# Two seams between three stages: a lasting staging buffer, an earlier load, batch norm in two steps, and a last group copied on chip

## The chip, the cores and the metric

The kernel runs on one core of a Trainium2 chip. A core has five engines with instruction streams of their own: PE (TensorE, matmuls; PEld is its weight load), DVE (VectorE), ACT (ScalarE), POOL (GpSimd) and SP (SyncE, which here only issues DMAs). Sixteen DMA engines move data between DRAM and SBUF. Matmul results go to PSUM. The metric is the device time of one execution in microseconds; the median of several runs is compared.

## The reference, cut to what matters

The input x is 16 x 192 x 64 x 64 in float32. A first block and a second layer are computed; all is float32.

```
h = layer_norm(x over channels)
projected, gate = split(conv1x1(h))            # 192 -> 2 * 192
projected = depthwise3x3(projected, dw_k)
scanned = mix of four decaying scans of projected (left, right, down, up)
local = depthwise3x3(projected, le_k)
mixed = (scanned + local) * sigmoid(gate)
bn = batch_norm(mixed over all images and pixels, per channel)
x = x + conv1x1(gelu(bn))
x = x + fc2(gelu(fc1(layer_norm(x))))          # 192 -> 768 -> 192
wt = tap weights from relu(batch_norm(mean(x over pixels) @ w1)) @ w2
out = depthwise3x3(x, wt per image and channel; 4 taps) + bias
```

The batch norm needs sums over all 16 images, so nothing after it can start for a channel before the gate product of that channel is complete for the whole batch. That divides the kernel into stages.

## The kernel before, in words

**Three stages.** Stage A (`n` from 0 to 63, `project` on line 471) normalizes and projects. A chunk is 512 pixels of an image pair; four chunks are a block, of which there are 16. It writes projected values and gates of a block into a staging buffer, 48 KB per partition, of which there are two (`stg`, line 427) used in turn. The values are stored to DRAM (`pg_d`, line 81) sorted by channel group, 24 groups of 8 channels; the groups are divided into four tensors (`PARTS`, line 46). Group 0 is copied straight into an SBUF buffer that stays (`pg_even`, `store_first`, line 495). While block b is projected, one part of block b-1 is stored in each of its four chunks (lines 535 to 540); the last block is stored after the loop (lines 548 to 551).

Stage B (lines 554 to 740) works by group, four channel pairs to a group, 96 pairs `k` in all. `load_pg` (line 568) brings a group of 4 MB into one of three buffers: `pg_even` for groups 0, 3, 6, ..., `pg_o0` for 1, 4, ... and `pg_o1` for 2, 5, .... For each pair, `depthwise` (line 579, PE) multiplies by banded matrices `dm`, `tables` and `scans` (ACT, DVE) run the vertical scans, `local` and `vertical` (PE, through `lmul`, line 629, with matrices `lm`) do the rest, and `gate` (line 659, DVE) multiplies by the sigmoid, overwrites the group's buffer and collects statistics by `bn_stats`. After a group's last pair, POOL stores the group to DRAM (`mixed_d`, line 673).

`batch_norm` (line 677) turns the statistics into a scale and a bias, for channels 0 to 127 at `k` = 76 and for 128 to 191 at the end. It has two halves: PE sums the means over partitions (`pm`), DVE forms squared deviations (`dv`); then PE sums these (`pq`), and DVE and ACT form scale and bias.

Stage C (line 969 on) works by chunks `n` of 512 pixels of an image pair. `load_y` (line 198) reads the gated values back from `mixed_d`; three pieces `t` (channels 0 to 127 of either image, and 128 to 191 of both). `unmix` (line 794) transposes them on DVE into `mx`, two buffers used in turn, `bn_gelu` (ACT) applies scale, bias and gelu, `out_proj` (PE, then DVE on line 827) adds the projection to x in the image buffer `ximg`; `center`, `squares` and `normalize` do the second layer norm, `first` and `second` the two fully connected layers. The first step is `n` = -3: a chunk is unmixed three steps before its `first`.

**Order.** Inside each stage the order of the instructions on every engine, SP's and POOL's DMA issues among them, is the order of the program text (`manual_schedule`). An engine runs its instructions in that order, and one that waits holds those behind it. Waits come from the data: a load of `mixed_d` waits for the store, a write into a buffer waits for what still reads it.

**Memory.** Buffers of an ended stage give their place to later ones. `pg_o0` lies on stage A's weights and inputs, `pg_o1` on a staging buffer; `wf2` (fc2's weights, line 100) holds stage A's raw weights until then; `ximg` lies on buffers of stage B.

Of the kernel before, what the change touches and what calls it, by code (L numbers as in the profile page):

```python
# [27 lines left out]
C = 192  # L28
HW = 64
# [16 lines left out]
PARTS = ((1, 6), (6, 12), (12, 18), (18, NCG))  # L46
# [8 lines left out]
def conv_block_kernel(ctx: ExitStack, tc: tile.TileContext, x, prm, w_in, w_out, w_fc1, b_fc1, w_fc2, w1, bn1, w2, out):  # L55
# [44 lines left out]
    wf2 = k2.tile([128, NFC, C], F32, tag="wf2", name="wf2")  # L100
# [72 lines left out]
    mats[0]["lm"] = lm_even  # L173
    bn_sc = cp.tile([128, 2], F32, tag="bn_sc", name="bn_sc")
# [9 lines left out]
    def load_lm(g):  # L184
        n = GC // 2
        for i, q in enumerate(HALF):
            v = lv_d[g, i, :, 0:1, :]
            src = bass.AP(v.tensor, v.offset, [[n, HW], [128 * n, 5], [1, HW * n]])
            (nc.sync, nc.gpsimd)[i].dma_start(mats[g % 2]["lm"][q].rearrange("p k m c -> p k (m c)"), src)
# [8 lines left out]
    def load_y(n, y, queues, ts=(0, 1, 2)):  # L198

        p, c = divmod(n, NCH)
        for t, q, i, c0 in ((0, slice(0, 128), 0, 0), (1, slice(0, 128), 1, 0), (2, HALF[0], 0, 128), (2, HALF[1], 1, 128)):
            if t in ts:
                nq = (q.stop - q.start) // 32
                ih, i8 = divmod(2 * p + i, n_half)
                v = mixed_d[i8, c // 2, HALF[ih]].rearrange("w g e -> w (g e)")[:, c0 * BR:(c0 + 32 * nq) * BR]
                for wh in range(2):
                    vw = v[32 * wh:32 * wh + 32].rearrange("w (q e) -> q w e", q=nq)
                    qd, k = (q, wh) if t < 2 else (HALF[wh], i)  # L210
                    if len(queues) == 1:
                        queues[0].dma_start(y[qd, t, k], vw)
                    else:
                        for b in range(nq):
                            p0 = qd.start + 32 * b
                            queues[b % 2].dma_start(y[p0:p0 + 32, t, k], vw[b])


    with ExitStack() as stage:
# [5 lines left out]
        w0 = wf2.rearrange("p m c -> p (m c)").rearrange("p (t n) -> p t n", t=3)  # L225
# [190 lines left out]
        for k in range(5):  # L416
            beside(40 + k, load_weights, k)
        beside(46, load_dm, 0)
        beside(47, load_lm, 0)
        beside(48, load_dm, 1)  # L420
        beside(50, lambda: finish_weights(0, bank()))
# [5 lines left out]
        stg = [stage.enter_context(tc.tile_pool(name=f"stg{i}", bufs=1)) for i in range(2)]  # L427
# [43 lines left out]
        def project(n):  # L471
            blk, part = divmod(n, per)
            if part == 0:
                both_i = stg[blk % 2].tile([128, 2, 2 * C, BR], F32, tag="stg", name="stg")
                stag[blk] = [both_i[:, i] for i in range(2)]
            for g in range(AR):
                ps = [psa.tile([128, 2 * C], F32, tag=f"pj{i}", name=f"ps_pj{i}", bufs=2) for i in range(2)]
                for t in range(3):
                    for i, q in enumerate(HALF):
                        nc.tensor.matmul(ps[i], pixels(n, t, g)[q], wi[q, t].rearrange("p g k c -> p (g k c)"),  # L480
                                         start=(t == 0), stop=(t == 2))
                if n + 1 < n_ac:
                    variance(n + 1, g)
                j, rs = part * AR + g, ast[n]["rs"]
                nc.vector.tensor_scalar_mul(stag[blk][0][:, :, j], ps[0], rs[:, g, 0:1])  # L485
                nc.scalar.activation(stag[blk][1][:, :, j], ps[1], AF.Copy, scale=rs[:, g, 1:2])  # L486
# [8 lines left out]
        def store_first(blk):  # L495

            for i, par, q, i8, b, qh in each(blk):
                (nc.gpsimd, nc.sync)[par].dma_start(pg_even[qh, i8 * NB + b].rearrange("p k c j -> p (k c j)"),
                                                    stag[blk][i][q, 0:2 * GC].rearrange("p o j -> p (o j)"))
# [7 lines left out]
        with tc.manual_schedule(engines=ORDER):  # L507
# [23 lines left out]
            for n in range(n_ac):  # L531
                if n + 3 < n_ac:
                    load_a(n + 3)
                blk, part = divmod(n, per)
                if blk:
                    if part == 0:
                        store_first(blk - 1)
                    store(blk - 1, part, (nc.gpsimd, nc.sync))
                    if part == per - 1:
                        stag.pop(blk - 1)  # L540
                if n + 1 < n_ac:
                    turn(n + 1)
                project(n)
                if n + 1 < n_ac:
                    deviation(n + 1)
                for f, args in side.pop(n, ()):
                    f(*args)
            store_first(blk)
            store(blk, 0, (nc.gpsimd, nc.sync))
            for d in range(1, len(PARTS)):  # L550
                store(blk, d, (nc.gpsimd, nc.gpsimd))


    with ExitStack() as stage:
        pg_odd = []
        kb = stage.enter_context(tc.tile_pool(name="kb", bufs=1))
        pg_odd.append(kb.tile([128, n_blk, 2, GC, BR], F32, tag="pg_o0", name="pg_o0"))
        wb = stage.enter_context(tc.tile_pool(name="wb", bufs=2))
        kc = stage.enter_context(tc.tile_pool(name="kc", bufs=1))
        late = {}  # L560
# [7 lines left out]
        def load_pg(g):  # L568
            s = grp[g]
            if g == 2:  # L570
                pg_odd.append(kc.tile([128, n_blk, 2, GC, BR], F32, tag="pg_o1", name="pg_o1"))
            s["pg"] = pg_even if g % 3 == 0 else pg_odd[g % 3 - 1]
            if g:
                d = [lo_ <= g < hi_ for lo_, hi_ in PARTS].index(True)
                lo_ = (g - PARTS[d][0]) * GE
                nc.sync.dma_start(s["pg"].rearrange("p n k c j -> p n (k c j)"),
                                  pg_d[d][:, :, :, lo_:lo_ + GE].rearrange("i b p e -> p (i b) e"))
# [51 lines left out]
        def lmul(k, m, src, dst, start, stop):  # L629
            g, c = divmod(k, hp_)  # L630
            for i, q in enumerate(HALF):
                for ih, o in enumerate(HALF):
                    nc.tensor.matmul(dst(bst[k]["ps"][i][o]), mats[g % 2]["lm"][q, m, :, c], src(q, ih), start=start, stop=stop)  # L633
# [25 lines left out]
        def gate(k):  # L659
# [10 lines left out]
            if c == hp_ - 1:  # L670

                for i0, i1 in ((0, n_half),) if g < NCG - 1 else ((0, 2), (2, n_half)):
                    nc.gpsimd.dma_start(mixed_d[i0:i1, :, :, g].rearrange("i b p e -> p (i b) e"),
                                        s["pg"][:, i0 * NB:i1 * NB, 0].rearrange("p n c j -> p n (c j)"))
                s.clear()

        def batch_norm(cls):

            chs = (slice(0, 128), slice(128, C))[cls]
            n = chs.stop - chs.start  # L680

            means = stats.rearrange("p c (e k) -> p k e c", k=3)[:, 1, :, chs]
            sums2 = stats.rearrange("p c (e k) -> p k e c", k=3)[:, 2, :, chs]
            dv = late["dev"][:, :, chs]
# [6 lines left out]
            nc.vector.scalar_tensor_tensor(dv, sums2, 2.0 / (n_half * HW), dv, ALU.mult, ALU.add)  # L691
            pq = psb.tile([128, CH], F32, tag="l", name="pq", bufs=4)
# [12 lines left out]
        with tc.manual_schedule(engines=ORDER):  # L705
            load_pg(0)
            load_pg(1)
            load_pg(2)
            mats[1]["lm"] = kc.tile([128, 5, HW, hp_], F32, tag="lm1", name="lm1")
            load_lm(1)  # L710
            late["dev"] = kc.tile([128, 2, C], F32, tag="dev", name="dev")
            for k in range(-2, n_bp + 1):
                if 0 <= k + 1 < n_bp:
                    tables(k + 1)
                if k >= 1:
# [3 lines left out]
                    if c == 0 and 0 < g < NCG - 1:  # L719
                        load_lm(g + 1)  # L720
                    if c == 0 and g + 2 < NCG:
                        load_pg(g + 2)
# [9 lines left out]
                if k == n_bp - 5 * hp_:  # L732
                    batch_norm(0)
# [5 lines left out]
            load_y(0, y_low, (nc.sync, nc.gpsimd), (2,))  # L739
            batch_norm(1)  # L740

# [52 lines left out]
    def unmix(n):  # L794

        c, y = n % NCH, ys[n // 2]
        mx = mxs[n % 2]
        r0 = (c % 2) * CR
        for t in range(3):

            kinds = ("p k (c j) -> p j k c", "p (r k w) -> p r k w") if t < 2 else ("p k (c j) -> p k j c", "p (k r w) -> p k r w")
            blocks = y[:, t].rearrange(kinds[0], j=BR)
            blocks = blocks[:, r0:r0 + CR] if t < 2 else blocks[:, :, r0:r0 + CR]
            nc.vector.transpose(mx[:, t].rearrange(kinds[1], k=2, w=32), blocks)  # L804
        st[n].update(mx=mx)
# [153 lines left out]
    def at(f, n, *a):  # L959
        if 0 <= n < n_ch:  # L960
# [8 lines left out]
    with tc.manual_schedule(engines=ORDER):  # L969
        for n in range(-3, n_ch + 1):  # L970
# [3 lines left out]
            if n == -3:  # L974
                border(ximg[0])
                nc.vector.memset(pool2, 0.0)
            if n == NCH - 3:
                border(ximg[1])
            at(load, n + 3)
            at(unmix, n + 3)  # L980
            at(load_mixed, n + 4)
            at(first, n, 0)
            at(bn_gelu, n + 3)
# [21 lines left out]
            at(second, n, 1)  # L1005

# [51 lines left out]
```

## Time and profile before

| | |
|---|---|
| median of 4 runs | 3883.9 us (3878.66 to 3886.72) |
| profiled execution | 3884.27 us |
| its span, first to last instruction | 3882.5 us |
| PE busy | 3793.3 us (98%) |
| DVE busy | 2596.9 us (67%) |
| ACT busy | 1775.1 us (46%) |
| POOL busy | 412.8 us (11%) |
| mean granted PE clock | 0.989 |

The profile records one execution. Times below are microseconds from the start of its span. A line such as `L589` is line 589 of the kernel; `ps_d<-pg_o,dm` is what an instruction writes and reads. In lists of waits, the engine that waits and its line come first, then what it waited for: total time, how many times, the longest. In lists in order of time, the columns are start, duration, engine, line, operation, `x` and the number of instructions merged, and in brackets the idle time before them with what ended it.

### The profile page before, as it was taken

What the parts mean: (1) busy time and instruction counts of PE and PEld (TensorE: products, weight loads), DVE (VectorE), ACT (ScalarE), POOL (GpSimd) and SP (SyncE); (2) the same over time, 40 slices, a digit from 0 to 9 for tenths busy, and PEclk for the clock granted to TensorE, in tenths of its full rate; (3) what the DMA queues carried; (4) which work ended last, traced back from release to release, by engine and by line L of the source; (5) the groups of instructions that cost most, each with busy time, mean ns of one, the idle gap of its engine ahead of it and who ended that gap; (6) DMA issues with size and microseconds to landing.
All of it is one profiled execution on the core that took longest, in us unless ns stands there. A gap on an engine that the chain in (4) does not pass through costs nothing.

```text
span 3882.5 us, 59908 instructions
## 1 busy us (share of the span) xinstructions
PE 3793.3 (98%) x24972; PEld 1728.6 (45%) x24972; DVE 2596.9 (67%) x3820; ACT 1775.1 (46%) x1879; POOL 412.8 (11%) x667
## 2 busy tenths in 40 slices
PE   8999999999999989999999999999999999999998
PEld 5566665555555433333333333333333333333333
DVE  6777777899999954446656656655665665664654
ACT  3333334788887733334333433433433433343432
POOL 2333332001010020000000000000000000000000
PEclk9999999999999989999999999999999999999999
DMA  6789987999999841112212212222222221221212
GB/s 156 228 246 245 276 256 256 256 283 274 279 278 254 215 87 35 39 41 66 80 44 67 69 59 63 60 64 59 68 55 63 71 63 44 80 70 41 68 28 71
DMA packets 305535, 491.03 MB, mean 126 GB/s; under 512 B 45344, under 2 KB 200208, under 8 KB 305264
## 3 DMA queue, kind: packets, MB, share of 16 engines
q1 hardware_dynamic: 246640, 290.58, 27.9%
q0 software_dynamic: 58208, 196.28, 18.8%
q8 instruction: 197, 3.23, 0.4%
q14 instruction: 74, 0.61, 0.1%
q10 hardware_dynamic: 416, 0.33, 0.0%
HBM read 284.98 MB, written 197.92 MB: 124 GB/s over the span
## 4 chain that ended last, share of the span: by engine, by line
PE 92%; DMA 4%; DVE 2%; issue 1%; ACT 0%; SPq 0%; POOL 0%; DVEq 0%; POOLq 0%; ACTq 0%
PE ps_f L870 27%; PE ps_f L775 25%; PE ps_pj L480 11%; PE ps_l L633 10%; PE ps_d L589 6%; PE ps_o L824 5%; PE ps_o L820 3%; PE ps_xt L455 2%; PE ps_v L775 1%; PE ps_m L775 1%; DMA pg_d<-stg 1%; DMA pg_o<-pg_d 1%; DMA dm<-dv_d 1%; DMA xa<-in_x_dram 1%; DMA out_dram<-ol 0%
## 5 line engine op out<-in xcount | busy, mean ns | idle before, releaser
L870 PE MATMUL ps_f<-h,wf 64*128 64x512 f32 x4608 | 1042.5, 598 | 3.1 <-DVE h L860 3.1
L775 PE MATMUL ps_f<-gl,wf 128*64 128x512 f32 x4608 | 1021.5, 592 | 0.0
L873 ACT ACTIVATE gl<-ps_f,bf 128x1024 f32<-128x1024 f32 x384 | 428.2, 1115 | 1182.9 <-PE ps_f L870 1182.1
L870 PEld LDWEIGHTS ps_f<-h,wf 64*128 64x128 f32 x4608 | 430.6, 187 | 611.8 <-issue 611.0
L827 DVE SCALAR_TENSOR_TENSOR ximg<-ps_o,pt,low 128x256 f32<-128x256 f32 x384 | 168.3, 480 | 748.6 <-PE ps_o L824 748.6
L775 PEld LDWEIGHTS ps_f<-gl,wf 128*64 128x64 f32 x4608 | 330.5, 137 | 580.0 <-issue 537.9
L480 PE MATMUL ps_pj<-wi,xa 64*128 64x384 f32 x3072 | 516.9, 489 | 5.8 <-DVE stg L485 5.7
L486 ACT ACTIVATE stg<-ps_pj,rsa 128x384 f32<-128x384 f32 x256 | 239.0, 939 | 377.3 <-PE ps_pj L480 347.5
L480 PEld LDWEIGHTS ps_pj<-wi,xa 64*128 64x128 f32 x3072 | 292.3, 188 | 202.6 <-issue 12.3
L67 DVE SCALAR_TENSOR_TENSOR o<-ximg,taps,o 128x1024 f32<-128x1024 f32 x252 | 323.5, 1284 | 84.9 <-ACT o L930 78.8
L934 POOL DMA_DIRECT2D out_dram<-o x168 | 88.2, 530 | 2158.0 <-DVE o L67 2155.4
L485 DVE TENSOR_SCALAR stg<-ps_pj,rsa 128x384 f32<-128x384 f32 x256 | 228.3, 892 | 103.0 <-PE ps_pj L480 85.6
L859 DVE RECIPROCAL rs<-rs 128x512 f32<-128x512 f32 x64 | 214.6, 3353 | 82.6 <-ACT rs L858 82.6
L624 DVE TENSOR_TENSOR_SCAN v<-tab,q 128x1024 f32<-128x1024 f32 x96 | 218.3, 2274 | 10.8 <-ACT tab L612 10.8
L626 DVE TENSOR_TENSOR_SCAN v<-tab,q 128x1024 f32<-128x1024 f32 x96 | 217.5, 2265 | 0.0
L824 PE MATMUL ps_o<-low,wo 128*64 128x256 f32 x1536 | 210.2, 395 | 0.0
L612 ACT ACTIVATE tab<-mask,dec_b 128x1024 f32<-128x1024 f32 x192 | 209.3, 1141 | 0.0
L891 DVE SCALAR_TENSOR_TENSOR ximg<-ps_f,pt,ximg 128x512 f32<-128x512 f32 x192 | 137.4, 749 | 92.3 <-PE ps_f L775 88.0
L589 PE MATMUL ps_d<-pg_o,dm 64*64 64x384 f32 (+2 forms) x2560 | 181.2, 426 | 14.9 <-DMA pg_o<-pg_d 14.6
L462 DVE BATCH_NORM_STATS2 st<-ps_xt 128x6 f32<-128x192 f32 x512 | 174.1, 340 | 24.0 <-PE ps_xt L455 24.0
L589 PEld LDWEIGHTS ps_d<-pg_o,dm 64*64 64x64 f32 x2560 | 123.4, 198 | 103.4 <-issue 75.2
L804 DVE STREAM_TRANSPOSE low<-low 128x512 f32<-128x512 f32 x174 | 167.4, 1015 | 0.0
(181 smaller groups left out, 3710.1 us busy)
## 6 DMA issues: line engine op xcount, KB each, us to landing
pg_o<-pg_d SPq DMA_DIRECT2D x16, 4096.0 KB
low<-in_x_dram SPq DMA_DIRECT2D x128, 384.0 KB
out_dram<-o POOLq DMA_DIRECT2D x168, 256.0 KB, 3.7
pg_d<-stg POOLq DMA_DIRECT2D x102, 384.0 KB, 7.5
pg_d<-stg SPq DMA_DIRECT2D x90, 384.0 KB
mixed_d<-pg_o POOLq DMA_DIRECT2D x15, 2048.0 KB, 11.8
low<-mixed_d SPq DMA_DIRECT2D x116, 256.0 KB
low<-pg_d SPq DMA_DIRECT2D x7, 4096.0 KB
```

The lines of the kernel that those rows point to most:

```text
L67: nc.vector.scalar_tensor_tensor(o, in0, scalar, in1, ALU.mult, ALU.add, **kw)
L480: nc.tensor.matmul(ps[i], pixels(n, t, g)[q], wi[q, t].rearrange("p g k c -> p (g k c)"), start=(t == 0), stop=(t == 2))
L485: nc.vector.tensor_scalar_mul(stag[blk][0][:, :, j], ps[0], rs[:, g, 0:1])
L486: nc.scalar.activation(stag[blk][1][:, :, j], ps[1], AF.Copy, scale=rs[:, g, 1:2])
L589: nc.tensor.matmul(dst(ps[o, ih]), mats[g % 2]["dm"][q, di + 1, :, ch], src(s["pg"][q, :, 0, ch]), start=(di == 0), stop=stop)
L624: nc.vector.tensor_tensor_scan(vf, tab, q, 0.0, ALU.mult, ALU.add)
L626: nc.vector.tensor_tensor_scan(vf[:, ::-1], tab[:, ::-1], q[:, ::-1], 0.0, ALU.mult, ALU.add)
L633: nc.tensor.matmul(dst(bst[k]["ps"][i][o]), mats[g % 2]["lm"][q, m, :, c], src(q, ih), start=start, stop=stop)
L775: nc.tensor.matmul(ps[q], w(i), rhs(i), start=start, stop=stop)
L824: nc.tensor.matmul(ps[q, wh].rearrange("p (r w) -> p r w", w=32), wo[:, 64 * t:64 * t + 64], cols(rows(s["mx"][:, i]))[:, :, wh], start=Fa ...
L870: nc.tensor.matmul(pf[:, i], wf1[q, t, 128 * m:128 * m + 128], s["h"][q, t], start=(t == 0), stop=(t == 2))
L873: nc.scalar.activation(gl, pf, AF.Gelu, bias=bf1[:, m:m + 1])
```

## The change

1. **Staging.** A buffer `mid` (48 KB per partition) lasts through stages A and B. It takes the blocks with odd numbers; even ones keep a buffer of stage A. In stage B, `mid` holds the buffer of groups 2, 5, 8, ... (formerly `pg_o1`), the `lm` matrices of odd groups and `dev`, the batch norm's deviations. The last group, 23, therefore lies in `mid`, and `ximg[0]` of stage C lies over it.
2. **Parts.** Group 1 becomes a part of its own: `PARTS` has five tensors. While the next block is projected, group 1 is stored with the first rows, and one of the other four parts in each chunk.
3. **Second group's load.** Of the last block only the first rows and group 1 are stored inside stage A, by POOL and ACT. Stage B then begins with `load_pg(1)`, images 0 to 5 of either half on SP and the rest on POOL; the other 16 stores of the last block follow on SP, then `load_pg(2)`.
4. **lm of group 1.** It is loaded during stage A into `place`, the memory that holds stage A's raw weights before and fc2's weights later; these are loaded at group 3.
5. **Batch norm.** `batch_norm` is split into `spread` (pm and dv) and the rest, which follows one pair later for the first 128 channels.
6. **End of stage B.** The transposes of chunk 0 move from stage C to the end of stage B, around `spread(1)` and `batch_norm(1)`. Chunk 0's third piece is read from DRAM without the last group, two pairs before the end; the last group's rows are copied from its SBUF buffer into `y_low` by four DMAs. The last group is stored with one DMA instead of two.
7. **Start of stage C.** The memset of `pool2` moves from `n` = -3 to `n` = 0. The transposes and the gelu of chunk 2 move from the start of step `n` = -1 to its end.

```diff
-PARTS = ((1, 6), (6, 12), (12, 18), (18, NCG))
+PARTS = ((1, 2), (2, 7), (7, 13), (13, 18), (18, NCG))
...
+    place = k2.tile([128, 5 * HW * (GC // 2)], F32, tag="place", name="place")
+    wf2 = place[:, 0:NFC * C].rearrange("p (m c) -> p m c", m=NFC)
...
+    SB_ = 2 * 2 * C * BR
+    mid = ce.tile([128, SB_], F32, tag="mid", name="mid")
+    mats[1]["lm"] = mid[:, NPG:NPG + 5 * HW * (GC // 2)].rearrange("p (k m c) -> p k m c", k=5, m=HW)
...
+    lm_first = place.rearrange("p (k m c) -> p k m c", k=5, m=HW)
+    lm_of = lambda g: lm_first if g == 1 else mats[g % 2]["lm"]
...
+                    if last < 32:
+                        for b, ncb in ((0, 32), (1, last)):
+                            p0 = qd.start + 32 * b
+                            queues[0].dma_start(y[p0:p0 + 32, t, k, 0:ncb * BR], vw[b, :, 0:ncb * BR])
...
+    def turn_back(y, mx, half, t):
+        kinds = ("p k (c j) -> p j k c", "p (r k w) -> p r k w") if t < 2 else ("p k (c j) -> p k j c", "p (k r w) -> p k r w")
+        blocks = y[:, t].rearrange(kinds[0], j=BR)
+        r = slice(half * CR, (half + 1) * CR)
+        nc.vector.transpose(mx[:, t].rearrange(kinds[1], k=2, w=32), blocks[:, r] if t < 2 else blocks[:, :, r])
...
-        for k in range(5):
+        for k in (0, 1, 3, 4):
             beside(40 + k, load_weights, k)
...
+        beside(49, load_lm, 1)
...
-                both_i = stg[blk % 2].tile([128, 2, 2 * C, BR], F32, tag="stg", name="stg")
+                if blk % 2:
+                    both_i = mid.rearrange("p (i o j) -> p i o j", i=2, j=BR)
+                else:
+                    both_i = stg.tile([128, 2, 2 * C, BR], F32, tag="stg", name="stg")
...
                     if part == 0:
                         store_first(blk - 1)
-                    store(blk - 1, part, (nc.gpsimd, nc.sync))
+                        store(blk - 1, 0, (nc.gpsimd, nc.sync))
+                    store(blk - 1, part + 1, (nc.gpsimd, nc.sync))
...
-            store_first(blk)
-            store(blk, 0, (nc.gpsimd, nc.sync))
-            for d in range(1, len(PARTS)):
-                store(blk, d, (nc.gpsimd, nc.gpsimd))
+            store_first(blk, (nc.gpsimd, nc.scalar))
+            store(blk, 0, (nc.gpsimd, nc.gpsimd))
...
-                for i0, i1 in ((0, n_half),) if g < NCG - 1 else ((0, 2), (2, n_half)):
-                    nc.gpsimd.dma_start(mixed_d[i0:i1, :, :, g].rearrange("i b p e -> p (i b) e"),
-                                        s["pg"][:, i0 * NB:i1 * NB, 0].rearrange("p n c j -> p n (c j)"))
+                if g == NCG - 1:
+                    for i in range(2):
+                        for wh in range(2):
+                            w0_ = 32 * wh
+                            (nc.sync, nc.gpsimd)[wh].dma_start(y_low[2 * w0_ + 32:2 * w0_ + 64, 2, i, LASTC * BR:],
+                                                              s["pg"][w0_:w0_ + 32, i * NB, 0].rearrange("p c j -> p (c j)"))
+                nc.gpsimd.dma_start(mixed_d[:, :, :, g].rearrange("i b p e -> p (i b) e"),
+                                    s["pg"][:, :, 0].rearrange("p n c j -> p n (c j)"))
...
             load_pg(0)
-            load_pg(1)
+            load_pg(1, nc.sync, 0, n_half - 2)
+            load_pg(1, nc.gpsimd, n_half - 2, n_half)
+            for d in range(1, len(PARTS)):
+                store(blk, d, (nc.sync, nc.sync))
             load_pg(2)
...
+                    if c == 0 and g == 3:
+                        load_weights(2)
...
                 if k == n_bp - 5 * hp_:
+                    spread(0)
+                if k == n_bp - 5 * hp_ + 1:
                     batch_norm(0)
...
-            load_y(0, y_low, (nc.sync, nc.gpsimd), (2,))
+                if k == n_bp - hp_ // 2:
+                    load_y(0, y_low, (nc.sync,), (2,), LASTC)
+            turn_back(y_low, mxs[0], 0, 0)
+            spread(1)
+            turn_back(y_low, mxs[0], 0, 1)
             batch_norm(1)
+            turn_back(y_low, mxs[0], 0, 2)
...
+            if n == 0:
                 nc.vector.memset(pool2, 0.0)
...
+            early_, late_ = (n + 3, None) if n != -1 else (None, 2)
             at(load, n + 3)
-            at(unmix, n + 3)
+            at(unmix, early_)
...
-            at(bn_gelu, n + 3)
+            at(bn_gelu, early_)
...
             at(second, n, 1)
+            at(unmix, late_)
+            at(bn_gelu, late_)
```

## The prediction

> **What bounds the kernel now.** I began with busy time by stage, cutting the span at the two seams (columns: length, then busy time and instruction count of PE, PE's weight loads, DVE, ACT, POOL; granted PE clock, DMA share, GB/s).
>
> ```profile
> 0.00:648.80 648.80, 625.67 (x3966) 392.45 (x3966) 478.37 (x1491) 250.73 (x336) 218.48 (x367) 1.00 0.85 233
> 648.80:1353.70 704.90, 675.48 (x7692) 374.44 (x7692) 668.34 (x584) 572.09 (x677) 79.25 (x85) 0.98 0.99 266
> 1353.70:1392.90 39.20, 18.95 (x126) 8.24 (x126) 25.00 (x37) 12.15 (x12) 21.50 (x37) 0.67 0.86 186
> 1392.90:3882.50 2489.60, 2473.24 (x13192) 953.43 (x13192) 1425.19 (x1709) 940.12 (x854) 93.54 (x179) 1.00 0.22 58
> ```
>
> The first and last rows are PE without gaps (626 of 649, 2473 of 2490 us): nothing but PE work could change them. The middle stage has PE and DVE close together, and the 39 us before the last stage are less than half filled. So I asked PE's waits, longest first:
>
> ```profile
> PE ps_d L589 <- DMA pg_o<-pg_d: 14.6, 1, 14.6
> PE ps_o L820 <- ACT low L810: 10.6, 1, 10.6
> ...
> PE pq L696 <- DVE dev L691: 6.3, 2, 5.6
> PE ps_v L775 <- DVE sm_sq L850: 5.6, 1, 5.6
> ```
>
> Four holes, one or two each; all lie at seams or at the batch norm. For the middle stage I then read DVE in order of time, since there a hole counts only if DVE, too, stands still:
>
> ```profile
> 679.99 2.27 DVE L626 TENSOR_TENSOR_SCAN v<-tab,q 128x1024 f32<-128x1024 f32 x1
> 697.59 0.69 DVE L667 TENSOR_TENSOR low<-ps_l,sg 128x512 f32<-128x512 f32 x1 [15.34 <-PE ps_l L633]
> ...
> 1204.33 2.27 DVE L624 TENSOR_TENSOR_SCAN v<-tab,q 128x1024 f32<-128x1024 f32 x1
> ...
> 1211.33 2.27 DVE L624 TENSOR_TENSOR_SCAN v<-tab,q 128x1024 f32<-128x1024 f32 x1
> ...
> 1224.77 2.27 DVE L624 TENSOR_TENSOR_SCAN v<-tab,q 128x1024 f32<-128x1024 f32 x1
> ...
> 1363.70 0.06 DVE L976 MEMSET pool<- 128x6 f32 x1 [5.23 <-DMA low<-mixed_d]
> 1363.80 5.66 DVE L804 STREAM_TRANSPOSE low<-low 128x512 f32<-128x512 f32 x6
> ```
>
> The scans start every 7.00 us (1204.33, 1211.33): that is DVE's period for a pair, without a gap, against PE's 6.89. DVE sets this stage; 96 x 7.00 = 672 us, and it lasts from 659.4 to 1353.7. The excess is the 15.34 us hole and the 13.44 us pair of the first batch norm (6.44 too long), with little else. At the second seam the last gate product ends at 1352.94, and DVE starts the transposes only at 1363.80, behind a memset that was let go with the last group's store. The chain of what ended last says where that time goes:
>
> ```profile
> 1353.26 7.82 DMA mixed_d<-pg_o x2
> 1361.08 4.16 DMA low<-mixed_d
> 1365.27 0.48 DVE low L804
> ```
>
> A round trip through DRAM, 12 us. The first hole has its own line on SP, whose load of group 1 waited for the last stores of that group:
>
> ```profile
> 649.81 1.23 SPq L504 DMA_DIRECT2D pg_d<-stg  x2
> 656.35 22.82 SPq L576 DMA_DIRECT2D pg_o<-pg_d  x2
> ```
>
> Issued at 656.35, it landed at 687.6, among the last block's stores (6.3 MB) and group 2's load.
>
> **What the skill says.** (1) "DMA: Bandwidth & Descriptors", section on the anatomy of one DMA: a DMA costs about 2.0 us plus bytes at 436 GB/s, most of the fixed part being the receipt of the last write. Trace: the 64 KB first-rows copies at 649.43 took 2.39 us; agrees. (2) Same page, "Issuing engines are not separate DMA queues": SP, ACT and POOL share the 16 engines, so moving stores from POOL to SP buys no bandwidth and costs none. Trace: SP's load alone moves 348 GB/s (687 to 694 us), both queues' stores about 370 (615 to 632); roughly agrees. (3) "TensorE: Matmul & The Clock Gate", section on the HAM clock gate: idle PE falls to half clock and needs about 3.4 us of work to recover. Trace: after the first hole 40 L589 matmuls took 5.36 us, elsewhere 2.61; agrees. DVE's 15.34 us already contain this.
>
> **The change, part by part.**
>
> *Group 1 ahead of the last stores.* Three quarters of the load (images 0 to 5 of each half, 3 MB) need nothing of the last block and only the memory of stage A's inputs, free at 648.7. It can go at about 649.3. Its own last stores (256 KB, POOL) land near 655, then POOL loads the last 1 MB. With 4.5 MB at some 350 GB/s (the rate of the seam between 652 and 694 us) that is 13 us: landed near 664. PE asks at 673.1 (687.73 - 14.6), DVE stalls only if depthwise(4) starts after 675.3 (scan 3 ends at 682.2, less 6.9 us of PE work before the next gate). Margin 11 us: gain 15.3.
>
> What is late next: group 2. Behind group 1 on SP stand 16 stores (5.8 MB), then group 2's load, which overwrites `mid` and so waits for all of them. 649.3 + (3 + 1 + 0.5 + 5.8 MB)/356 GB/s = 678; 2 us receipt; 4 MB at 348 = 11.5, 2 more: 694, or 697 if dm's halves come between. dm for group 2 follows on SP at about 698. PE asks at 673.1 + 27.6 = 700.7, DVE suffers from 703.3. Cover 3 to 7 us; I take 0, bounds 0 and +10. Group 3 comes after the store of group 0 (693 + 13), landed by 720, needed at 731. Hidden.
>
> *Staging, five parts.* 16 blocks x 4 = 64 more stores, half of them per queue: 2 x 0.61 us on SP and 2 x 0.55 on POOL in the first chunk of a block. SP is busy 8.7 us there (299.48 to 308.2), so about 9.9 against a chunk of 9.4, but its x loads are three chunks ahead. Same bytes; the last part's size and issue time, on which the buffer's return depends, stay. The load of lm for group 1 moves into stage A (0.65 MB), fc2's weights (0.59 MB, 1.7 us of DMA) move to group 3, behind about 10 us of slack. The first rows go by POOL and ACT instead of POOL and SP: ACT is idle until 656.75. All 0; bounds -2 and +8.
>
> *First batch norm in two steps.* Now PE waits 5.6 us for dv, and starts cold: two vertical passes took 3.70 instead of 1.89 us. With the pq products one pair later, PE goes on with vertical(76) and depthwise. DVE keeps the three dv operations (0.57 + 0.43 + 0.61, with gaps 1.75) and the five small ones (mv to bias: 0.16 + 0.36 wait + 4 x 0.2 = 1.3). Sum 3.1, and 0.1 of queueing: 3.2 instead of 6.44. Gain 3.2, bounds 1.5 and 4.7 (6.44 - 1.75: only dv left).
>
> *Second seam.* Counted from the end of the gate: statistics end at 1353.67; transpose t0 to 1354.65 (0.94 each, 6 in 5.66) while PE makes pm (ends 1354.9); dv 1354.94 to 1356.06 as before; t1 to 1357.1 beside pq; mv 1357.2, square root on ACT, scale and bias ready at 1358.47; t2 1358.5 to 1359.5. The four copies of 16 KB on chip, on SP and POOL, start at 1353.3; by (1) 2.04 us, say landed by 1356.5: no wait, and 2 us of cover. Group 22's rows are loaded long before. ACT: gelu table loaded at 1359.0, 1.2 us for t0 and t1, 0.8 for t2: PE starts at 1361.0 instead of 1367.78. Gain 6.8. Chunk 2's three transposes (2.9 us) leave the stretch between chunk 0's sums and its centering; PE's own order gives back 0.6 of it: gain 2.3. Then they stand behind normalize, beside 7 us of first(0,0); ACT takes chunk 2's gelu first, which may hold out_proj(2) by 0.4. Against it: `mid` now holds the last group and ximg[0] lies on it. The first write of ximg[0] (L827) would be ready at 1364.1; the store, issued at 1354.4 after POOL's two copies, lands some 10 us later (2 MB in 10.3 us before): 1364.4. Loss 0.3, bounds 0 and 4. Sum 6.8 + 2.3 - 0.4 - 0.3 = 8.4.
>
> *Sum.* 15.3 + 3.2 + 8.4 = 26.9 off 3882.5 us of span: 3855.6. The profiled execution took 3884.27 (1.8 around the span), 0.4 above the median of 3883.9, so **3857** for the median. The last stage is PE without gaps and passes the gain on.
>
> **Rivals.** *Group 2 late.* For: 0.99 DMA share, everything behind 16 stores on one queue, cover of 3 to 7 us. Against: 350 GB/s on that queue. If it lands at 708 to 713, 5 to 10 us are lost: 3862 to 3867. *The last stage pinned by ximg[0].* For: the memset at 1363.70 shows that a new buffer over the last group's memory waits for its store, and such stores took up to 13.7 us under load. Then L827 starts at 1368: 3861. *The early load isn't early*: it still waits for the last stores, because something of theirs lies in its memory or the load isn't split from them. Only 11.6 remain: 3872. *Slower: stage A's block boundaries.* A new block may write its staging only when the stores of two blocks ago have landed; at 292.10 such a store took 11.9 us against a lead of 9.4, and PE lost 1.1 us. Four more stores in a block, queued on SP ahead of the x loads and of later stores, could stretch this. Over 15 boundaries it decides from 26.9/15 = 1.8 us more each; at 2.5 us each the time is 3857 + 37 = 3894. Against: the stores that decide go out three chunks after the added ones, and from 530 us on boundaries cost nothing (9.40 us for each chunk).
>
> **How the numbers follow.** Forecast 0.62; group 2 late 0.13; pinned start 0.10; load not early 0.05; stage A longer 0.10, of which 0.07 end slower and 0.03 level. Faster 0.90, same 0.03, slower 0.07; a change under 0.2% (8 us) is about what a measurement of this kernel can't tell from none. The range: down, 5 us beyond the forecast's gains (its bounds: 1.5 at the batch norm, 2 in stage A, the rest at the seams) and 2 for the spread of runs, 3850; up to 3868, which takes in the first two rivals. That holds about 0.82.
>
> **What would show it.** Right: no wait of L589 for pg_o near 675, scans every 7 us through groups 1 and 2; the batch-norm pair near 10.2 us; 8 us from the last gate product to out_proj, 31 to first(0,0). Wrong: L589 waiting at the start of group 2; L827 waiting for the store; stage A over 650 us; a load of group 1 that starts after 655.

## The result: three gains arrived, two new waits took them back

The kernel after takes 3886.43 us (median, 3880.29 to 3891.55) against 3884.02 us (3877.62 to 3892.33) for the kernel before in the same comparison: a ratio of 1.0005, 95% interval 1.000 to 1.001. Nothing was gained. The forecast was 3857.

The totals hide that much moved. Five marks that every trace here has cut the span: the last block of stage A (start of PE's first depthwise matmuls), the first scan on DVE, the moments' matmul `pm` that follows the last gate product, the first matmul of `first(0, 0)`, and the end.

| us | stage A | last block to first scan | stage B: first scan to `pm` | `pm` to `first(0,0)` | to the end | span |
|---|---|---|---|---|---|---|
| before | 648.76 | 10.65 | 694.41 | 39.04 | 2489.64 | 3882.5 |
| after | 648.83 | 17.33 | 693.79 | 31.48 | 2489.97 | 3881.4 |
| forecast | 648.8 | 10.65 | 675.9 | 30.6 | 2489.6 | 3855.6 |

The forecast's row is the row of before less 15.3 and 3.2 in stage B and 8.4 at the second seam. Stage A and stage C are as foreseen. The first seam is 6.7 us too long, stage B 17.9 and the second seam 0.9. The table also makes the experiments readable: the stretch called stage A differed between 644.7 and 655.1 us from one execution to the next, also in kernels whose stage A is the same, so effects of a few microseconds are read below from a stretch and not from the whole time.

**The hole before group 1 is gone.** DVE's scans in order of time in the kernel after (start, duration, engine, line), where before had its wait of 15.34 us at 682.2:

```profile
677.54 2.27 DVE L648 TENSOR_TENSOR_SCAN v<-tab,q 128x1024 f32<-128x1024 f32 x1
...
684.54 2.28 DVE L648 TENSOR_TENSOR_SCAN v<-tab,q 128x1024 f32<-128x1024 f32 x1
...
691.54 2.27 DVE L648 TENSOR_TENSOR_SCAN v<-tab,q 128x1024 f32<-128x1024 f32 x1
...
698.55 2.27 DVE L648 TENSOR_TENSOR_SCAN v<-tab,q 128x1024 f32<-128x1024 f32 x1
```

A pair every 7.00 us, also where group 1 begins (its first gate product is at 702.92) and, further on, group 2, which came in time. The first batch norm, same view, answers to before's 7.00, then 13.44:

```profile
1202.68 2.27 DVE L648 TENSOR_TENSOR_SCAN v<-tab,q 128x1024 f32<-128x1024 f32 x1
...
1211.35 2.27 DVE L648 TENSOR_TENSOR_SCAN v<-tab,q 128x1024 f32<-128x1024 f32 x1
...
1219.53 2.27 DVE L648 TENSOR_TENSOR_SCAN v<-tab,q 128x1024 f32<-128x1024 f32 x1
...
1226.53 2.27 DVE L648 TENSOR_TENSOR_SCAN v<-tab,q 128x1024 f32<-128x1024 f32 x1
```

Two pairs of 8.67 and 8.18 us: 2.85 us more than two plain pairs, where before had 6.44 and 0.14 more. A gain of 3.7.

**Two new waits.** The list of PE's waits after (what waits, for what: total, times, longest) has two that before had not:

```profile
PE ps_l L657 <- DVE pg_o L691: 12.8, 1, 12.8
PE ps_d L613 <- DMA pg_d<-mid: 8.4, 1, 8.4
...
PE ps_o L857 <- ACT low L847: 5.4, 1, 5.4
```

The first is in stage B, at the start of group 22, the last but one. DVE's instructions there, in order of time:

```profile
1289.55 2.27 DVE L648 TENSOR_TENSOR_SCAN v<-tab,q 128x1024 f32<-128x1024 f32 x1
1291.74 2.27 DVE L650 TENSOR_TENSOR_SCAN v<-tab,q 128x1024 f32<-128x1024 f32 x1
1310.56 1.03 DVE L240 STREAM_TRANSPOSE low<-low 128x512 f32<-128x512 f32 x1 [16.55 <-DMA low<-mixed_d]
1311.52 0.65 DVE L691 TENSOR_TENSOR pg_o<-ps_l,sg 128x512 f32<-128x512 f32 x1
...
1314.13 2.27 DVE L648 TENSOR_TENSOR_SCAN v<-tab,q 128x1024 f32<-128x1024 f32 x1
...
1332.50 1.04 DVE L240 STREAM_TRANSPOSE low<-low 128x512 f32<-128x512 f32 x1
```

L240 is `turn_back`, a transpose that brings gated values into stage C's layout. The kernel's text has chunk 0's three behind the last gate product, and that is where four more run, from 1359.72 on. So the two here are taken to be chunk 1's, which the kernel's text has in stage C (`unmix(1)`, step `n` = -2); e1 below bears this out. Here one stands between a pair's scans and its gate product, and waits 16.55 us for a load of gated values; the chain of what ended last gives that load, and the store that it waited for:

```profile
1289.38 11.76 DMA mixed_d<-low
1301.22 0.64 SPq L228
1301.92 8.51 DMA low<-mixed_d
```

From scan to scan 24.58 us went by (1289.55 to 1314.13) instead of 7.00: 17.6 lost. The second transpose costs its own 1.0.

The second wait is at the first seam. All engines and queues in order of time:

```profile
648.71 1.28 ACTq L526 DMA_DIRECT2D low<-mid  x2
648.79 0.40 SPq L600 DMA_DIRECT2D pg_o<-pg_d  x1
...
648.83 1.14 PE L613 MATMUL ps_d<-low,dm 64*64 64x512 f32 x4 [1.12 <-ACT mid L514]
648.97 1.06 POOL L526 DMA_DIRECT2D low<-mid  x2 [28.28 <-DVE mid L513]
649.24 19.06 SPq L532 DMA_DIRECT2D pg_d<-mid  x10
...
658.32 9.85 PE L613 MATMUL ps_d<-low,dm 64*64 64x512 f32 x110 [8.36 <-DMA pg_d<-mid]
```

L526 are the four copies of the last block's first rows, 64 KB each, that group 0 needs; L600 on SP is the 3 MB load of group 1, now issued at the same moment. PE waits 8.36 us where it waited 2.22 before, and the first scan comes at 666.16 instead of 659.41. (The wait is put down to a store that ended about then; PE needs the copies. POOL's two landed 5.9 and 7.1 us after issue, the later at 656.6; for ACT's two the views give no landing.)

At the second seam, ACT's order differs from the one in the prediction:

```profile
1363.18 1.24 ACT L846 ACTIVATE low<-low,bn_bi,bn_sc 128x1024 f32<-128x1024 f32 x1 [4.23 <-DVE low L240]
...
1364.44 1.28 ACT L733 ACT_TABLE_LOAD   x1
1365.74 0.30 ACT L733 ACTIVATE bn_sc<-mv,eps 128x1 f32<-128x1 f32 x1
1366.05 1.28 ACT L847 ACT_TABLE_LOAD   x1
...
1368.66 1.13 PE L857 MATMUL ps_o<-low,wo 64*64 64x256 f32 x8 [5.35 <-ACT low L847]
```

The gelu of chunk 0's first two pieces (L846, written in stage C) runs ahead of the batch norm's square root (L733, stage B), and the function table is loaded twice between it and the next gelu: three loads at this seam, where before had two. `out_proj` starts 9.59 us after the last gate product (1359.07), instead of 14.84 before and 8.06 forecast.

### The profile page after: what moved, and what is told of

The parts are those of the page before. It is cut to its first block, busy times and chain, and to the rows that moved or that the text cites. A ratio compares the mean times of both kernels' runs of the same rounds, so it can differ in the third digit from the quotient of the medians.

```text
span 3881.4 us, 59952 instructions
## 1 busy us (share of the span) xinstructions
PE 3801.0 (98%) x24972; PEld 1807.9 (47%) x24972; DVE 2598.4 (67%) x3820; ACT 1780.0 (46%) x1880; POOL 422.5 (11%) x685
## 4 chain that ended last, share of the span: by engine, by line
PE 84%; issue 11%; DMA 2%; DVE 2%; POOL 1%; ACT 0%; SPq 0%; POOLq 0%; DVEq 0%; ACTq 0%
PE ps_f L907 26%; PE ps_f L819 25%; PE ps_pj L508 12%; PE ps_o L861 5%; PE ps_l L657 4%; PE ps_o L857 3%; PE ps_d L613 2%; PE ps_xt L480 2%; PE ps_v L819 1%; PE ps_m L819 1%; DMA out_dram<-ol 0%; DMA mixed_d<-low 0%; PE ps_k L819 0%; DVE ol L67 0%; DMA pg_d<-stg 0%
## 5 line engine op out<-in xcount | busy, mean ns | idle before, releaser
L819 PE MATMUL ps_f<-gl,place 128*64 128x512 f32 x4608 | 1021.5, 592 | 0.0
L819 PEld LDWEIGHTS ps_f<-gl,place 128*64 128x64 f32 x4608 | 330.5, 137 | 580.0 <-issue 537.9
L648 DVE TENSOR_TENSOR_SCAN v<-tab,q 128x1024 f32<-128x1024 f32 x96 | 218.3, 2274 | 17.5 <-DMA pg_d<-mid 17.5
L514 ACT ACTIVATE stg<-ps_pj,rsa 128x384 f32<-128x384 f32 x128 | 119.8, 940 | 193.5 <-PE ps_pj L508 183.5
L514 ACT ACTIVATE mid<-ps_pj,rsa 128x384 f32<-128x384 f32 x128 | 120.5, 942 | 182.8 <-PE ps_pj L508 170.5
L240 DVE STREAM_TRANSPOSE low<-low 128x512 f32<-128x512 f32 x174 | 168.0, 1016 | 17.2 <-DMA low<-mixed_d 16.5
L468 POOL DMA_DIRECT2D xa<-in_x_dram x192 | 120.6, 634 | 369.9 <-PE ps_pj L508 310.4
L657 PE MATMUL ps_l<-q,low 64*64 64x504 f32 (+1 forms) x1152 | 147.8, 597 | 12.8 <-DVE pg_o L691 12.8
```

The source lines that it names most:

```text
L648: nc.vector.tensor_tensor_scan(vf, tab, q, 0.0, ALU.mult, ALU.add)
L657: nc.tensor.matmul(dst(bst[k]["ps"][i][o]), lm_of(g)[q, m, :, c], src(q, ih), start=start, stop=stop)
L819: nc.tensor.matmul(ps[q], w(i), rhs(i), start=start, stop=stop)
```

## The experiments

"First scan" below is the stretch from the last block to it, as in the table.

### What put the transposes into stage B

The change moves chunk 1's transposes nowhere. But it moves the memset of `pool2`, the first DVE instruction of stage C, from `n` = -3 to `n` = 0. In before, that memset waited until 1363.70 with the transposes behind it. The theory: it was this memset that kept them out of stage B. Three kernels test it.

**e1** writes chunk 1's transposes at the end of stage B's block (and leaves them out of `unmix`), the memset where the change put it.

```diff
             turn_back(y_low, mxs[0], 0, 2)
+            for t in range(3):
+                turn_back(y_low, mxs[1], 1, t)
...
-        for t in range(3 if n else 0):
+        for t in range(3 if n > 1 else 0):
```

> The changed kernel with one edit: chunk 1's three transposes, which opened DVE's work of stage C, are written at the end of stage B, behind chunk 0's. Theory (the compiled order put them inside stage B once the memset no longer stood ahead of them, and there DVE waited 16.5 us for their input): stage B has no such hole, the last gate product ends near 1340.7 instead of 1359.1, the three transposes (3 us) hide behind PE's first out_proj (4 us of DVE wait there), and the time falls by about 18 us, to 3868. Rival (the hole is a late load of the gated values, and whatever comes next on DVE would have waited for it): the wait turns up behind the last gate or at another instruction, and the time stays at 3886.

**e2** puts only the memset back to `n` = -3.

```diff
                 border(ximg[0])
-            if n == 0:
                 nc.vector.memset(pool2, 0.0)
```

> The changed kernel with one edit undone: the memset of pool2 is back at the first step of stage C. Theory (it was this memset that kept the transposes of stage C out of stage B): the hole in stage B is gone as in the run before; chunk 1's transposes now follow the memset, which may wait for memory of stage B: 3868 if it waits for nothing late, up to 3874 if it waits for the last group's store. Rival (the memset has nothing to do with it): the hole stays, 3886.

**e3** is the other way round: the kernel before, with only the memset moved to `n` = 0.

```diff
                 border(ximg[0])
+            if n == 0:
                 nc.vector.memset(pool2, 0.0)
```

> The kernel before with this part of the change alone: the memset of pool2 moved from the first step of stage C to step 0. Theory: two transposes (chunk 0's first two pieces) move into stage B and DVE waits there for the load of the gated values, as in the changed kernel: a hole of about 16 us, plus table loads on ACT between sigmoids; at the second seam two transposes less (2 us) and no wait of the memset: 3884 + 17.5 - 2 = about 3899, range 3892 to 3904. Rival (the memset only waited, and moving it is free): 3880 to 3884.

Measured: e1 3863.57 us, ratio 0.9956 (0.9941 to 0.9971); e2 3864.11, ratio 0.9957 (0.9943 to 0.997); e3 3902.91, ratio 1.0058 (1.0045 to 1.0072). Stage B takes 675.24 us in e1 and 675.25 in e2, 18.5 less than in after, and 717.21 in e3, 22.8 more than in before. (e1 and e2 lie some 4 us below the times that were expected, since the kernel before itself measured 3880.26 us in that comparison and not 3883.9.) DVE in e2, in order of time:

```profile
1319.76 2.27 DVE L648 TENSOR_TENSOR_SCAN v<-tab,q 128x1024 f32<-128x1024 f32 x1
1326.76 2.27 DVE L648 TENSOR_TENSOR_SCAN v<-tab,q 128x1024 f32<-128x1024 f32 x1
1336.40 1.03 DVE L240 STREAM_TRANSPOSE low<-low 128x512 f32<-128x512 f32 x1
```

No transpose before the last gate product, which ends at 1335.76. So e1's rival, by which any instruction that came next would have waited for that load, has fallen: in e1 and e2 the wait turns up nowhere else in stage B. In e3 (before's line L804 is the transpose of `unmix`, L624 a scan):

```profile
1295.72 2.27 DVE L624 TENSOR_TENSOR_SCAN v<-tab,q 128x1024 f32<-128x1024 f32 x1
1318.52 1.04 DVE L804 STREAM_TRANSPOSE low<-low 128x512 f32<-128x512 f32 x1 [18.34 <-DMA low<-mixed_d]
1326.17 1.03 DVE L804 STREAM_TRANSPOSE low<-low 128x512 f32<-128x512 f32 x1 [4.72 <-DMA low<-mixed_d]
1327.70 2.27 DVE L624 TENSOR_TENSOR_SCAN v<-tab,q 128x1024 f32<-128x1024 f32 x1
```

From scan to scan 31.98 us go by instead of 7.00, a hole of 25.0, since both transposes wait; 17.5 had been expected. Stage B grows by less, because this execution's wait for group 1 was 13.1 us and not 15.34.

What follows: the place of one line, a memset of 0.06 us, decides over 18.5 us of stage B in the kernel after and 22.8 in the kernel before. `manual_schedule` fixes the order inside one stage's block; an instruction of the next block can still be emitted among those of this one. Written into the block of stage B (e1), the same transposes stay at its end. By which rule the order across blocks is made, these runs don't show.

### Batch norm alone

**e4** is the kernel before with only the batch norm split.

```diff
                 if k == n_bp - 5 * hp_:
+                    spread(0)
+                if k == n_bp - 5 * hp_ + 1:
                     batch_norm(0)
```

> The kernel before with the batch norm in two steps alone. Theory: the pair of the first batch norm takes 2.9 us too long, spread over two pairs, instead of 6.6: 3880.3, that is 3.7 us or 0.1% less. Rival (stage B's end is set by loads that fill the gain again): 3884.

Measured: 3877.12 us, ratio 0.999 (0.9984 to 0.9997). The scans around it start at 1208.18, 1215.18, 1223.86 and 1232.04: two pairs take 8.68 and 8.18 us, as in after. The median is 3.1 us below that of before. Stage B takes 688.24 us, 6.2 less than before, of which 2.4 are another thing: this execution's wait for group 1 was 12.90 us and not 15.34. That leaves 3.7 for the split, which is what after shows.

### What delays group 0

Theory: the 3 MB load, issued together with the copies, takes the DMA engines from them. All kernels here build on e1, so that stage B is clean.

**e5** issues all four copies on SP, ahead of the load; **e6** two on POOL and two on SP, as before had them.

e5:

```diff
-            store_first(blk, (nc.gpsimd, nc.scalar))
+            store_first(blk, (nc.sync, nc.sync))
```

> The kernel of e1 (chunk 1's transposes kept out of the middle of stage B), with one edit more: all four copies of the last block's first rows are issued by SP, just ahead of group 1's load, instead of two by POOL and two by ACT beside it. Theory (the 3 MB load that SP issues first takes the DMA engines, and the 64 KB copies on the two other queues share with it): ahead of the load on its own queue the copies land within 3 to 4 us, group 0's first scan starts at 660 to 661 us instead of 666, everything later moves up by about 5 us, and the time is 5 us below that of e1 (ratio to before 0.9943 to 0.9947). Rival (the copies are slow for another reason, such as the eviction that they wait for or the stores behind them): the first scan stays near 666 and the time is that of e1. Second rival (the earlier start is given back, since group 1 or 2 then comes late): the first scan moves, but a hole of 4 to 5 us opens before group 1 or 2 and the time is that of e1.

e6:

```diff
-            store_first(blk, (nc.gpsimd, nc.scalar))
+            store_first(blk, (nc.gpsimd, nc.sync))
```

> The kernel of e1 with the first rows' copies on POOL and SP, as in the kernel before: SP's two are ahead of the load on its queue, POOL's two still run beside it. Theory (sharing with the load): POOL's two copies stay late, landing after about 6 us or more as they do in e1, so the first scan comes at 662 to 666 us and the time is 0 to 3 us below e1's. Rival (only the two on ACT were late, by ACT's own queue): the first scan comes at 660 to 661, as in e5, and the time is 5 us below e1's.

Measured: e5 3860.19 us (3856.23 to 3864.08), ratio 0.9948 (0.9935 to 0.996), first scan after 12.60 us. e6 3855.70 us (3854.46 to 3858.35), ratio 0.9937 (0.9925 to 0.995), first scan after 10.47 us, against 16.39 in e1 and 10.65 in before. e5 gains 3.8 of the 5 expected, since SP takes 2.65 us to issue four copies one after the other. Stage B stays at 675.2 in both, so no later group pays for it. The expectation of e6 missed: POOL's two copies weren't late at all, they landed 2.5 us after issue. That spoke for the rival, a slow queue of ACT. But e6 also issues the load later, behind SP's two copies:

```profile
647.53 1.12 SPq L526 DMA_DIRECT2D low<-mid  x2
647.65 1.14 PE L613 MATMUL ps_d<-low,dm 64*64 64x512 f32 x4 [1.04 <-ACT mid L514]
647.79 1.06 POOL L526 DMA_DIRECT2D low<-mid  x2 [27.95 <-DVE mid L513]
...
649.00 0.49 SPq L600 DMA_DIRECT2D pg_o<-pg_d  x1
...
651.05 9.04 PE L613 MATMUL ps_d<-low,dm 64*64 64x512 f32 x110 [2.27 <-DMA low<-mid]
```

Two more kernels part the load's moment from ACT's queue. **e8** is e6 with the load on ACT, where nothing is ahead of it; **e9** is e1 with all four copies on POOL and the load first on SP, so that ACT issues nothing.

e8, against e6:

```diff
-            load_pg(1, nc.sync, 0, n_half - 2)
+            load_pg(1, nc.scalar, 0, n_half - 2)
```

> The kernel of e6 (first rows on POOL and SP), but group 1's 3 MB load is issued by ACT, with nothing ahead of it on that queue, so that it goes off together with the copies instead of 1.4 us behind the first of them. Measured as the time from stage A's last block (PE's first depthwise matmuls) to group 0's first scan, which was 10.65 us in before, 17.3 in after, 16.4 in e1 and 10.5 in e6. Theory (a load that goes off no later than the copies holds them up, on whatever queue): 15 to 17 us, PE's wait near 8. Rival (only copies issued by ACT are slow, by ACT's own queue): 10.5 us, PE's wait near 2.3. Theory and rival differ by about 6 us of the time (3862 against 3856).

e9, against e1:

```diff
-            store_first(blk, (nc.gpsimd, nc.scalar))
+            store_first(blk, (nc.gpsimd, nc.gpsimd))
```

> The kernel of e1 with all four copies of the first rows on POOL, none on ACT; the load stays first on SP. Theory (a load that goes off no later than the copies holds them up): 16 to 18 us from the last block's end to the first scan. Rival (only copies issued by ACT are slow): POOL issues four in about 2.1 us and the last lands 2.5 later, so the first scan comes after 12 to 13 us, as in e5.

Measured: first scan after 17.52 us in e8 and 16.99 in e9; PE's waits 8.99 and 7.76 us; the times 3862.33 us (3860.06 to 3867.36) and 3864.02 (3863.23 to 3864.32). In e8, the load goes off between the copies:

```profile
646.47 0.48 SPq L526 DMA_DIRECT2D low<-mid  x1
646.56 0.44 ACTq L600 DMA_DIRECT2D pg_o<-pg_d  x1
646.74 1.05 POOL L526 DMA_DIRECT2D low<-mid  x2 [28.26 <-DVE mid L513]
...
647.69 0.91 SPq L526 DMA_DIRECT2D low<-mid  x1
```

POOL's two copies stand as in e6, but landed 7.1 to 7.5 us after issue instead of 2.4 to 2.7; in e9, POOL's four took 5.7 to 7.4. So ACT's queue is not the cause: the rival fell, and the theory holds in a sharper form: what counts is whether megabytes have been issued by the time of the copy, by whichever engine. One thing blurs e8: one of SP's sixteen stores, of 320 KB, slipped between SP's two copies, at 647.00. POOL's first copy was issued ahead of it, at 646.74, and still took 7.1 us. The Trainium skill says as much: "DMA: Bandwidth & Descriptors", "Issuing engines are not separate DMA queues": DMAs of all issuing engines run on the same 16 engines and interleave there. The traces agree, with 2.5 us against 7 for 64 KB.

The turn can be seen within one queue. Behind its copies POOL issues four stores of 64 KB (L532), half a microsecond apart. In e6 the first, issued at 648.85, 0.15 us ahead of the load, landed after 2.3 us; the other three, issued from 649.37 on, took 6.2 to 6.5. In e10 it is 2.7 us against 5.9 to 6.4.

### The order on ACT at the second seam

**e7** is e5 with chunk 0's two gelu instructions written in stage B's block, behind `batch_norm(1)`; **e10** has the same edit on e6.

```diff
             turn_back(y_low, mxs[0], 0, 2)
+            gelu_of(mxs[0])
...
     def bn_gelu(n):
         mx = st[n]["mx"]
+        if n == 0:
+            return
```

> The kernel of e5 with chunk 0's two gelu instructions written at the end of stage B, behind the second batch norm, instead of at the head of stage C. Theory (in the kernel after, ACT ran a gelu of the first pieces ahead of the batch norm's square root, which cost two more table loads of 1.28 us and let VectorE wait for bn_sc): the square root comes first, out_proj starts 8 to 8.6 us after the last gate product instead of 9.6 to 10, and the time is 1 to 2 us below e5's. Rival (PE waits at that point for the moments or for the last copies, not for ACT's order): out_proj starts as late as in e5 and the time is the same.

> The kernel of e6 with chunk 0's gelu behind the batch norm as in e7: chunk 1's transposes at the end of stage B, first rows on POOL and SP ahead of the load, square root ahead of the gelu. Theory: the gains of e6 and e7 add, since they lie at different seams: first scan 10.5 us after the last block, out_proj 7.2 us behind the moments' matmul instead of 9.1; the time is 1 to 2 us below e6's, about 27 us below before (ratio 0.9930 to 0.9938). Rival (the 1.9 us are given back inside stage C): the time is that of e6.

ACT and PE in e7 (L737 is the square root, L725 the gelu):

```profile
1338.05 0.29 ACT L737 ACTIVATE bn_sc<-mv,eps 128x1 f32<-128x1 f32 x1 [4.57 <-DVE mv L735]
1338.36 1.28 ACT L725 ACT_TABLE_LOAD   x1
1339.65 1.24 ACT L725 ACTIVATE low<-low,bn_bi,bn_sc 128x1024 f32<-128x1024 f32 x1
...
1341.65 1.13 PE L866 MATMUL ps_o<-low,wo 64*64 64x256 f32 x8 [3.84 <-ACT low L726]
```

The square root first, one table load behind it. From `pm` to `out_proj` 7.18 us in e7 and 7.19 in e10, against 9.10 in e5 and 9.11 in e6; from `pm` to `first(0,0)` 30.07 and 29.92 against 31.98 and 31.96. They last, in part: the next batch of matmuls on that line comes 40.07 us after `pm` in e10 against 42.55 in e6, but 40.77 in e7 against 42.07 in e5, so 2.5 and 1.3 us are left of them. In times they don't show: e7 has 3856.17 us (3855.29 to 3857.76), 4.0 below e5, which is more than the edit can give. And e10 has 3858.13 us (3855.88 to 3864.52), ratio 0.9949 (0.9935 to 0.9962), on another chip than e6 and not below it, short of what was expected of it. The step is thus shown by the traces alone, and whether stage C gives it back, the rival of e10, the times don't settle.

## Why the prediction was wrong, and where it was right

**Failed: the order between the stages, 18.5 us.** The section on the second seam let the transposes start right behind the gate because the last group's rows no longer pass through DRAM, and took the memset of 1363.70 only for something that was "let go with the last group's store". That its move is itself an edit was not costed at all. It rested on the statement in the description that "inside each stage the order of the instructions on every engine ... is the order of the program text". That holds inside a stage; the memset stood at the border, where the program text doesn't decide. e1, e2 and e3 show it. None of the rivals was this: the rival with the wrong sign placed its loss in stage A.

**Failed: "The first rows go by POOL and ACT instead of POOL and SP: ACT is idle until 656.75. All 0".** The bounds given there, -2 and +8, were for all of the staging; this term alone measured 6.7 us (first scan after 17.33 us instead of 10.65). The step asked whether the issuing engine was free, not what the DMA engines were doing. The price used for the copies, 2.39 us, was measured in before with the first stores issued only behind them; beside the load that the change itself puts there, it was 5.9 and 7.1. The trace of before had the other price, too: between 300 and 620 us, where stage A's loads and stores are under way, the same copies on POOL (L498) took 4.4 to 8.1 us, 5.8 in the median. With that loss, the early load nets 15.3 - 6.7 = 8.6 us in after. e6 shows that both are to be had: the load 1.35 us behind the last block instead of with it, no delay for group 0 and none for group 1.

**A size off: the second seam.** Forecast 8.4; after gained 7.6, e1 7.1, e10 9.1. The term that failed is "square root on ACT, scale and bias ready at 1358.47 ... gelu table loaded at 1359.0": in after a gelu came first, two table loads of 1.28 us behind it, again an instruction of stage C among those of stage B. e7 and e10, with the square root first, start `out_proj` 8.06 and 8.07 us after the last gate product, as forecast, and e10's stretch from there to `first(0,0)` is 2.35 us shorter than before's, where 2.3 was forecast for chunk 2's transposes. The loss that was booked for the store into `mid`'s place (0.3) is not seen in after, where `out_proj`'s DVE part waited for PE only. In e7 it did wait for that store:

```profile
1345.85 0.88 DVE L873 SCALAR_TENSOR_TENSOR ximg<-ps_o,pt,low 128x256 f32<-128x256 f32 x2 [2.59 <-DMA mixed_d<-mid]
```

It came 4.20 us behind `out_proj` instead of 3.08 as in e6, yet `first(0,0)` came earlier by the 1.9 us given above. So the rival of a start pinned by `ximg[0]` is close, but `first(0,0)` doesn't show it.

**Right: the hole, 15.3.** The scans run on through group 1, and stage B without the stray transposes takes 675.2 us where the forecast had 675.9. The margin of 11 us was not there, though: POOL's last 1 MB, forecast to land near 664, waits for POOL's 64 KB stores, which land late like the copies. In e6 it landed at 669.12, and PE asked for group 1 at 671.02. **Right: group 2 in time**, in all nine kernels with the early load. **Right in kind: the batch norm**, 3.7 measured (after and e4) for 3.2, inside its bounds of 1.5 and 4.7. **Right: stage C passes on what it gets**, 2489.1 to 2490.1 us from `first(0,0)` to the end in after and all kernels built on it. **Not refuted: stage A at 0.** 648.83 against 648.76. The rival that put 27 us or more there is refuted: the stretch took 644.7 to 652.2 us in the nine kernels with the new staging and 645.4 to 655.1 in the three with the old. PE's waits between 200 and 640 us, where block boundaries would cost, add up to 2.0 to 6.5 us in the nine and 2.9 to 8.2 in the three. No run isolates the staging, so a cost of a few microseconds can't be excluded. (Two readings of the prediction were off, and no term rests on them: the 370 GB/s between 615 and 632 us are 337 over that whole window, and the 40 matmuls set against 5.36 us took 2.79 in the same view, not 2.61.)

With the three mends, e10's span is 3854.0 in the profiled execution, its fastest of five: against before 19.2 us less in stage B, 9.1 less at the second seam, 0.2 more at the first; 28.1 together, where the forecast had 26.9. e6, with two of them, is the fastest in time at 3855.70 us, and the forecast was 3857. That this is so near is in part luck: before had 3881.3 us in that comparison and not 3883.9, so the gain is 25.6. Still, the sum of the parts was sound for the change as meant; what the change as written did between its blocks, and to the copies beside its load, was not in it.

## What to carry to other kernels

An instruction at the border of two separately ordered blocks can be the only thing that holds the next block's instructions back; before it is moved, ask what stands behind it and whether that waits for data which is not there yet. In the trace, look for a line of the next stage inside the present one. When a large transfer is brought forward, list the small ones issued at the same moment and price them beside it, not alone, from a stretch of the trace that is as busy as the one they will meet; one or two microseconds between them may cost nothing and save several. Where executions vary in a stretch that the edit doesn't touch, compare stretch by stretch between marks.

## What was not expected of the hardware

A copy of 64 KB landed 2.4 to 2.8 us after issue when the megabytes were issued just behind it (e6, e10), and 5.7 to 7.5 us when they were issued just ahead of it or among the copies (after, e8, e9), no matter which engine issued the megabytes. A few tenths of a microsecond decide: 0.15 us ahead of the load a 64 KB store of POOL took 2.3 us, 0.37 us behind it 6.5 (e6). And stage A ended anywhere between 644.7 and 655.1 us in the twelve profiled executions, while the stretch from `first(0,0)` to the end lies between 2489.1 and 2490.1 us in eleven of them (2486.7 in e4). Part of stage A's variation is PE's waits between 200 and 640 us: they add up to 8.2 and 6.5 us in the two longest (e4, e5) and to 2.2 in the shortest (e2). What lengthens them was not looked into.
